# A cross-attention block: the projection's bias put into PSUM by ScalarE, and a new order of the first blocks

## The chip, the core and the metric

The kernel runs on one core of a Trainium2 chip. A core has five engines with a queue each: TensorE (PE; the loading of its stationary operand is shown as PEld), VectorE (DVE), ScalarE (ACT), GpSimd (POOL) and SyncE (SP), which here issues every DMA. Each works through its own instructions in order and waits on semaphores for the others. Matrix products land in PSUM, which has eight banks of 512 float32 per partition; everything else lies in SBUF. The metric is the device time of one launch in microseconds, the median over runs.

## The reference

Two inputs, x (16 batches of 1024 rows, 512 wide) and ctx (16 batches of 64 rows), are normalised and modulated by a conditioning vector, x then attends to ctx with 16 heads of 32, and the result is projected and added to x. All is float32.

```python
def _ada_ln(x, c, W_ss, b_ss):
    mu = mean(x); var = mean((x - mu) ** 2)
    h = (x - mu) / sqrt(var + EPS)
    scale, bias = split(silu(c) @ W_ss + b_ss, 2)
    return (1.0 + scale)[:, None, :] * h + bias[:, None, :]

xq  = _ada_ln(x_q, t_vec, Wss_q, bss_q)
xkv = _ada_ln(x_kv, t_vec, Wss_kv, bss_kv)
q = (xq @ Wq + bq).reshape(B, Lq, nh, dh)
kv = (xkv @ Wkv + bkv).reshape(B, Lkv, 2, nh, dh)
scores = einsum('bqhd,bkhd->bhqk', q, k) / sqrt(dh)
out = einsum('bhqk,bkhd->bqhd', softmax(scores), v)
return x_q + (out @ Wp + bp)
```

## The kernel before

The 16384 rows of x are 32 blocks of 512 rows, two to a batch; NB is 32. A block i goes through these steps, each a function of the kernel:

- `load_x(i)` and `load_residual(i)` bring x twice, into x_i for the normalisation and into r_i for the final sum.
- `q_stats` (DVE), `q_scale` (a square root on ACT, two small POOL operations) and `hidden` (ACT, L277) normalise x_i. `turn` (DVE, L414) transposes it in 32x32 squares into a tile ht, of which there is one, and `move` (16 DMAs, L427) puts the squares where the query product wants them, xt.
- `queries(i, o)` is one of four groups of the query product (PE, L462) into a PSUM bank; `queried` adds the bias on ACT (L479).
- `scores(i, z)` are score products of half of the keys (PE, L490) into two tiles of two banks each, tag "s", of which there are two in all. DVE takes maxima from them (L501), then ACT copies them to SBUF (L508); that frees them.
- `maxima` spreads the maxima over the rows (DVE, L522), `subtract` takes them off (L535, on POOL by default, 128x2048 for each half), `weights` is the exponential (ACT, L541), `sums` adds up (DVE, L546), `inverse` inverts and spreads, `divide` multiplies (POOL, L566).
- `mix` is the product of weights and values (PE, L586), `mixed` or `mixed_halves` its copy to SBUF (ACT, L606 or L654 and L655).
- The projection. Blocks 0 to 2 at first, and the last blocks, use `project` (PE, L613, a bank for each 128 rows) and `projected` (DVE, L626). Blocks 2 to 28 use seven products of halves (`product`, PE, L694) in place of eight, from sums of the rows (`row_sums` on DVE, `last_row_sum` on POOL) and of the weights (`weight_sums`, tile WT); they accumulate in banks 2 and 3 and are added to r in between (`added`, DVE, L708). `residual(i)` has added the projection's bias to r_i before that (POOL, L288, four additions of 128x512).

Four single banks are handed out in turn by `bank`, from the list `ring`; in the loop `ring` has two, and banks 2 and 3 belong to `product`. Two functions for keys and values (`context_features`, `keys`, `value_products`, `value_tiles`) run once for every two batches.

No scheduler moves anything: the order in each queue is the order in which the calls stand in the program. It has three parts: the way in, written out by hand to the products of block 2; a loop over i = 3 to 29, in which parts of blocks i - 2 to i + 3 alternate; and a tail for blocks 30 and 31. In the loop, after `mix(i - 1)` PE has `queries(i + 1, 1)`, then products 1 and 2 of block i - 1; ACT has `mixed_halves(i - 1)` and `hidden(i + 2, (2, 3))`, then the query evacuation.

Of the kernel before, what the change touches and what calls it, by code (L numbers as in the profile page):

```python
# [15 lines left out]
P = 128  # L16
# [4 lines left out]
def cross_attention_block(  # L21
# [319 lines left out]
    def value_products(b):  # L341

        xk = xk_tiles.pop(b)
        pv = bank(f"pv_{b}").rearrange("p (j z f) -> p j z f", j=2, z=2)
        for j in range(2):
            for z in range(2):
                at = j * LKV + z * HK
                for k in range(NC):
                    for c in range(NC):
                        nc.tensor.matmul(  # L350
                            pv[c * 32 : (c + 1) * 32, j, z, :],
                            lhsT=xk[:, k, at : at + HK],
                            rhs=w_kv_sb[:, k, H + c * P : H + (c + 1) * P],
                            start=(k == 0),
                            stop=(k == NC - 1),
                        )
        pv_tiles[b] = pv
# [41 lines left out]
    def query_weights(b):  # L399
        t = qpool.tile([P, NC, H], F32, tag="wq", name=f"wq_{b}")  # L400
        for c in range(NC):
            scale = ss["q"][:, c, b : b + 1]
            if b == 0 and c % 2:
                nc.vector.tensor_scalar_mul(t[:, c, :], w_q_sb[:, c, :], scale)
            else:
                nc.scalar.mul(t[:, c, :], w_q_sb[:, c, :], scale)
        wq_tiles[b] = t
# [119 lines left out]
    def maxima(i):  # L527

        m = small.tile([P, HPC * NJ], F32, tag="m", name=f"m_{i}")
        both(m, m_tiles.pop(i), ALU.max)  # L530
        mb_tiles[i] = spread(i, m, f"mb_{i}", other=i == NB - 1)
# [103 lines left out]
    def half_weights(k, o):  # L635
        return w_p_sb[:, k * HC : (k + 1) * HC, o * HO : (o + 1) * HO]

    def weight_sums():
        t1, t2, t3, t4 = (WT[:, j] for j in range(4))
        nc.vector.tensor_tensor(t1, half_weights(0, 1), half_weights(0, 0), ALU.subtract)  # L640
        nc.vector.tensor_tensor(t2, half_weights(1, 1), t1, ALU.subtract)
        nc.vector.tensor_tensor(t3, half_weights(1, 1), half_weights(0, 1), ALU.subtract)
        nc.vector.tensor_tensor(t4, half_weights(1, 0), t2, ALU.subtract)

    s1_tiles, s2_tiles = {}, {}

# [23 lines left out]
        a12 = half_rows(i, 0, 1)  # L670
        nc.gpsimd.tensor_tensor(a12, a12, s2_tiles[i], ALU.subtract)

    acc = {}

    def product(i, n):

        rows, cols = {
            1: (lambda: half_rows(i, 0, 0), half_weights(0, 0)),
            2: (lambda: half_rows(i, 0, 1), half_weights(1, 0)),
            3: (lambda: half_rows(i, 0, 1), half_weights(1, 1)),  # L680
            4: (lambda: half_rows(i, 1, 1), WT[:, 3]),
            5: (lambda: s1_tiles.pop(i), WT[:, 0]),
            6: (lambda: s2_tiles[i], WT[:, 1]),
            7: (lambda: half_rows(i, 1, 0), WT[:, 2]),
        }[n]
        rows = rows()
        k = 2 if n in (1, 6, 5, 3) else 3
        new = n in (1, 2, 7)
        if new:
            acc[k] = bank(f"pp_{i}_{n}", k)  # L690
        for t in range(2):
            for c in range(HC):

                nc.tensor.matmul(  # L694
                    acc[k][:, t * HO : (t + 1) * HO],
                    lhsT=rows[:, c, t * P : (t + 1) * P],
                    rhs=cols[:, c, :],
                    start=new and t == 0 and c == 0,
                    stop=c == HC - 1,
                    skip_group_check=True,  # L700
                )
# [37 lines left out]
    queries(0, 1)  # L739
    hidden(1, (2, 3))  # L740
    load_x(2)
    for h in range(2):
        scale_shift_rows("kv", h)
    turn(1, range(NT))
    move(1)
    load_x(3)
    load_residual(0)
    load_projection_bias()
    queries(0, 2)
    for h in range(2):  # L750
        scale_shift("kv", 2 * NC, h)
# [6 lines left out]


    scores(0, 0)  # L760
    residual(0)
    value_products(0)
    scores(0, 1)
    turn(2, range(NT))
    move(2)
    load_projection()
    load_context(2)
    load_x(4)
    load_residual(1)
    maxima(0)  # L770
    subtract(0, nc.vector, (0,))
    value_tiles(0)
    subtract(0, nc.vector, (1,))
    queries(1, 0)
    query_weights(1)
    weights(0, 0)
    queries(1, 1)
    weights(0, 1)
    sums(0, 0)
    queries(1, 2)  # L780
    sums(0, 1)
    queries(1, 3)
    inverse(0)
    divide(0)
    scores(1, 0)
    q_stats(3)
    queries(2, 0)
    q_scale(3)
    scores(1, 1)
    maxima(1)  # L790
    queries(2, 1)
    subtract(1)
    queries(2, 2)
    hidden(3, (0, 1))
    mix(0, apart=False)
    mixed(0)
    hidden(3, (2, 3))
    queries(2, 3, spare=True)
    turn(3, (0, 1))
    kv_stats(2)  # L800
    turn(3, (2, 3))
    move(3)
    q_stats(4)
    project(0, 0)
    weights(1, 0)
    sums(1, 0)
    weights(1, 1)
    project(0, 1)
    sums(1, 1)
    q_scale(4)  # L810
    kv_scale(2)
    residual(1)
    project(0, 2, later=True)


    load_x(5)
    scores(2, 0)
    projected(0, 2)
    context_hidden(2)
    inverse(1)  # L820
    divide(1)
    project(0, 3, later=True)
    scores(2, 1)
    projected(0, 3)
    maxima(2)
    queries(3, 0)
    hidden(4, range(NT))
    queries(3, 1)
    queries(3, 2)
    mix(1)  # L830
    mixed(1)
    turn(4, range(NT))
    load_residual(2)
    move(4)
    q_stats(5, (0, 1))
    subtract(2, nc.vector)
    weights(2, 0)
    q_stats(5, (2, 3))
    queries(3, 3)
    weights(2, 1)  # L840
    weight_sums()
    sums(2, 0)
    project(1, 0)
    sums(2, 1)
    inverse(2)
    divide(2)
    q_scale(5)
    residual(2, (0, 1))
    context_features(2)
    project(1, 1)  # L850
    query_weights(2)
    project(1, 2)

# [1 line left out]
    for i in range(3, NB - 2):  # L855
        nxt3 = i + 3 < NB
        kvb = i // 4 * 2 + 2
        kv = i % 4 if kvb < B else None
        if nxt3:
            load_x(i + 3)  # L860
        if kv == 0:
            load_context(kvb)
        if i > 3:
            added(i - 2, 5)
        scores(i, 0)
        if i > 3:
            product(i - 2, 4)
            added(i - 2, 4)
            product(i - 2, 3)
            added(i - 2, 3)  # L870
        else:
            project(i - 2, 3)
            ring[:] = [0, 1]
        scores(i, 1)
        maxima(i)
        subtract(i)
        queries(i + 1, 0)
        load_residual(i)
        hidden(i + 2, (0, 1))
        mix(i - 1)  # L880
        mixed_halves(i - 1)
        hidden(i + 2, (2, 3))
        if kv == 1:
            context_hidden(kvb)
        if nxt3:
            q_stats(i + 3)
        if kv == 0:
            kv_stats(kvb)
        row_sums(i - 1)
        turn(i + 2, range(NT))  # L890
        move(i + 2)
        if not nxt3:
            load_residual(NB - 1)
        queries(i + 1, 1)
        product(i - 1, 1)
        product(i - 1, 2)
        weights(i, 0)
        added(i - 1, 1)
        added(i - 1, 2)
        sums(i, 0)  # L900
        weights(i, 1)
        queries(i + 1, 2)
        last_row_sum(i - 1)
        if i == 3:
            residual(2, (2, 3))
        residual(i)
        product(i - 1, 6)
        product(i - 1, 7)
        sums(i, 1)
        added(i - 1, 6)  # L910
        inverse(i)
        added(i - 1, 7)
        divide(i)
        if nxt3:
            q_scale(i + 3)
        if kv == 0:
            kv_scale(kvb)
        if kv == 2:
            context_features(kvb)
        if kv == 3:  # L920
            keys(kvb)
        queries(i + 1, 3)
        if (i + 2) % BPB == 0 and i + 2 < NB:
            query_weights((i + 2) // BPB)
        if kv == 3:
            value_products(kvb)
            value_tiles(kvb)
        product(i - 1, 5)
# [95 lines left out]
```

## Time and profile before

| what | value |
|---|---|
| median of 3 runs (lowest, highest) | 1095.79 us (1092.36, 1096.22) |
| the profiled execution | 1097.9 us, span of its instructions 1096.1 us |
| mean granted TensorE clock in it | 0.997 |
| busy: PE, DVE, POOL, ACT | 1077.3, 881.9, 746.6, 634.0 us |
| additions of the bias to r, POOL L288 | 128 of 1332 ns, 165.1 us |
| exponential, ACT L541, 128x2048 | 64 of 1915 ns |
| copies of mixed rows, ACT L655, 128x512 | 27 of 596 ns |
| DMA | 145.36 MB, 39.4% of 16 engines' span |

The profile is of one execution. A page gives the busy time of each engine, the chain of work that ended last and the groups of instructions with the mean duration of one. An entry of a timeline has the start and the length in us, engine, line, operation, what it writes and reads, and in brackets the idle time before it and what ended it. Neighbouring instructions of one kind are one entry. An entry of the waits has the waiting engine and line, what it waited for, the sum in us, how often, and the longest. A line of the windows has the stretch, its length, and the busy time of PE, PEld, DVE, ACT and POOL (instructions in brackets), the granted TensorE clock, the share of the DMA engines and GB/s. "Idle" on PE is counted from the modelled end of a product, so a short delay between two products can stand there without a bracket.

### The profile page before, as it was taken

Reading aid. Unit: us, or ns where it says so; the run is one execution under the profiler, and the core shown is the slowest. Engines: PE = TensorE matmul, PEld = TensorE weight load, DVE = VectorE, ACT = ScalarE, POOL = GpSimd, SP = SyncE. Lnnn points to the kernel's source line nnn. Section 1 sums busy time; section 2 is a strip of 40 time slices with the busy share of each in tenths; the row PEclk is TensorE's granted clock in tenths of the full one; section 3 lists DMA queues with packets and bytes.
Section 4 is the critical chain, followed back from the end, with each engine's and each line's share of the span. In section 5 each row is a group of like instructions: output and inputs, shape, how many; then the busy total and the mean of one; then the engine's idle time right before and its main releaser. Section 6 shows DMA issues by size and latency. Waiting matters only on the chain.

```text
span 1096.1 us, 20360 instructions
## 1 busy us (share of the span) xinstructions
PE 1077.3 (98%) x8290; PEld 614.7 (56%) x8290; DVE 881.9 (80%) x1138; ACT 634.0 (58%) x752; POOL 746.6 (68%) x359
## 2 busy tenths in 40 slices
PE   6989999999999999999999999999999999999998
PEld 3533455556655557555566555656656556755533
DVE  4687986888788886898868888688887888697893
ACT  3646754657566573666736677365755657466430
POOL 0065396778857777688758878578875777858830
PEclk9989999999999999999999999999999999999999
DMA  9543333443424442344434434343342443333402
GB/s 354 176 156 107 117 124 126 155 154 116 126 99 145 143 154 88 116 149 141 140 121 138 133 119 140 137 151 119 117 142 105 148 154 131 101 109 102 137 30 87
DMA packets 80525, 145.36 MB, mean 133 GB/s; under 512 B 10504, under 2 KB 10656, under 8 KB 80432
## 3 DMA queue, kind: packets, MB, share of 16 engines
q1 hardware_dynamic: 80432, 144.07, 39.4%
q8 instruction: 65, 1.06, 0.4%
q14 instruction: 28, 0.23, 0.1%
HBM read 77.97 MB, written 33.55 MB: 102 GB/s over the span
## 4 chain that ended last, share of the span: by engine, by line
PE 96%; DVE 2%; DMA 1%; SPq 0%; issue 0%; ACT 0%; DVEq 0%
PE pq L462 40%; PE pp L694 30%; PE po L586 7%; PE ps L490 6%; PE pp L613 6%; PE pv L350 3%; PE pk L322 3%; DMA wss_q<-in_L_xcond_Wss_q_dram 1%; DVE s L535 1%; DVE l L546 0%; PE pss_q L217 0%; PE pkt L302 0%; PE pxt L439 0%; DVE m L501 0%; DVE ht L414 0%; DVE mb L522 0%
## 5 line engine op out<-in xcount | busy, mean ns | idle before, releaser
L462 PE MATMUL pq<-xt,wq 128*128 128x512 f32 x1024 | 468.5, 602 | 1.1 <-DVE vt L363 0.9
L535 POOL TENSOR_TENSOR s<-s,mb 128x2048 f32<-128x2048 f32 x56 | 253.7, 4555 | 154.9 <-DVE mb L522 152.9
L566 POOL TENSOR_TENSOR s<-s,vb 128x2048 f32<-128x2048 f32 x62 | 280.1, 4540 | 84.9 <-DVE vb L522 61.0
L462 PEld LDWEIGHTS pq<-xt,wq 128*128 128x128 f32 x1024 | 189.0, 191 | 246.3 <-issue 241.0
L508 ACT COPY s<-ps 128x1024 f32<-128x1024 f32 x128 | 129.8, 1014 | 195.6 <-DVE m L501 188.3
L479 ACT ACTIVATE qt<-pq,bqs 128x512 f32<-128x512 f32 x128 | 88.0, 689 | 161.7 <-PE pq L462 157.7
L708 DVE TENSOR_TENSOR r<-pp,r 128x512 f32<-128x512 f32 x189 | 126.4, 669 | 68.6 <-PE pp L694 65.9
L288 POOL TENSOR_TENSOR r<-r,b_p_sb 128x512 f32<-128x512 f32 x128 | 165.1, 1332 | 17.8 <-DMA b_p_sb<-in_L_xcond_bp_dram 15.4
L501 DVE TRANSPOSE_TENSOR_REDUCE m<-ps 128x32 f32<-128x1024 f32 x128 | 152.2, 1227 | 27.8 <-PE ps L490 27.8
L546 DVE TRANSPOSE_TENSOR_REDUCE l<-s 128x64 f32<-128x2048 f32 x64 | 146.6, 2300 | 5.5 <-ACT s L541 5.5
L694 PE MATMUL pp<-w_p_sb,ot 128*128 128x256 f32 x648 | 148.7, 379 | 0.0
L541 ACT ACTIVATE s<-s 128x2048 f32<-128x2048 f32 x64 | 122.4, 1915 | 34.2 <-POOL s L535 26.3
L694 PEld LDWEIGHTS pp<-w_p_sb,ot 128*128 128x128 f32 x648 | 123.1, 190 | 28.3 <-issue 6.5
L694 PE MATMUL pp<-WT,ot 128*128 128x256 f32 x432 | 104.9, 386 | 0.0
L694 PE MATMUL pp<-WT,s 128*128 128x256 f32 x432 | 102.8, 381 | 0.0
L694 PEld LDWEIGHTS pp<-WT,s 128*128 128x128 f32 x432 | 81.5, 190 | 32.2 <-issue 20.5
L277 ACT ACTIVATE x<-x,rstdq 128x512 f32<-128x512 f32 x128 | 97.1, 813 | 1.7 <-POOL rstdq L255 1.7
L694 PEld LDWEIGHTS pp<-WT,ot 128*128 128x128 f32 x432 | 79.8, 190 | 32.4 <-DVE r L708 16.8
L246 DVE BATCH_NORM_STATS2 bs<-x 128x6 f32<-128x512 f32 x128 | 84.3, 659 | 2.0 <-DMA x<-in_x_dram 2.0
L414 DVE STREAM_TRANSPOSE ht<-x 128x512 f32<-128x512 f32 x124 | 77.5, 679 | 6.6 <-ACT x L277 6.6
L490 PE MATMUL ps<-qt,kt 32*32 32x512 f32 x2048 | 77.6, 602 | 3.1 <-ACT s L508 2.0
L522 DVE STREAM_TRANSPOSE mb<-m 128x2048 f32<-128x2048 f32 x32 | 74.0, 2311 | 5.0 <-POOL s L566 1.7
(90 smaller groups left out, 887.9 us busy)
## 6 DMA issues: line engine op xcount, KB each, us to landing
x<-in_x_dram SPq DMA_DIRECT2D x32, 1024.0 KB, 5.7
r<-in_x_dram SPq DMA_DIRECT2D x32, 1024.0 KB, 5.4
xt<-ht SPq DMA_DIRECT2D x496, 64.0 KB, 2.0
out_dram<-r SPq DMA_DIRECT2D x54, 512.0 KB, 2.8
out_dram<-r SPq DMA_DIRECT2D x20, 256.0 KB, 2.0
wss_q<-in_L_xcond_Wss_q_dram SPq DMA_DIRECT2D x2, 1024.0 KB, 9.4
ctx<-in_ctx_dram SPq DMA_DIRECT2D x8, 256.0 KB, 5.7
wss_kv<-in_L_xcond_Wss_kv_dram SPq DMA_DIRECT2D x2, 1024.0 KB
```

The lines of the kernel that those rows point to most:

```text
L277: nc.scalar.activation(dst, src, AF.Identity, bias=rstd[:, 1, j : j + 1], scale=rstd[:, 0, j : j + 1])
L288: nc.gpsimd.tensor_add(r_tiles[i][:, t, :], r_tiles[i][:, t, :], b_p_sb)
L462: nc.tensor.matmul(pq.rearrange("p (g n) -> p g n", g=4), lhsT=wq_tiles[b][:, c, o * P : (o + 1) * P], rhs=xt[:, :, c, :], start=(c == 0), ...
L490: nc.tensor.matmul(pss[r // 2][32 * c : 32 * c + 32, r % 2, :], lhsT=kt[rows, c, z * HK : (z + 1) * HK], rhs=qt[rows, c, :], start=True, s ...
L501: nc.vector.tensor_reduce(m_tiles[i][:, z, 2 * e : 2 * e + 2, :], pss[e].rearrange("p r (j a) -> p r j a", a=32), AX.X, ALU.max, apply_tra ...
L508: nc.scalar.copy(s_sb[:, 2 * e : 2 * e + 2, :], pss[e])
L535: eng.tensor_tensor(s_tiles[i, z], s_tiles[i, z], mb_tiles[i], ALU.subtract)
L541: nc.scalar.activation(p, p, AF.Exp, scale=SCALE)
L546: nc.vector.tensor_reduce(l_tiles[i][:, z], s_tiles[i, z].rearrange("p r (j a) -> p r j a", a=32), AX.X, ALU.add, apply_transpose=True,)
L566: eng.tensor_tensor(s_tiles[i, z], s_tiles[i, z], vb, ALU.mult)
L694: nc.tensor.matmul(acc[k][:, t * HO : (t + 1) * HO], lhsT=rows[:, c, t * P : (t + 1) * P], rhs=cols[:, c, :], start=new and t == 0 and c == 0,
L708: nc.vector.tensor_add(r, acc[k].rearrange("p (t h) -> p t h", t=2), r)
```

## The change

In the loop, for i from 4 on, `biased(i - 1)` has ACT copy the bias into banks 2 and 3 before products 1 and 2, which then accumulate on it instead of opening their bank. Bank 2 gets the bias of the second half of the columns, twice side by side, and bank 3 the difference of the two halves, b_diff; what this leaves out is added to a quarter of r by `residual_rest` (POOL), one addition in place of four. Block 2's products, in the round i = 3, still open their banks (`first`), and blocks from 29 on keep `residual`.

The weights' sums and b_diff are computed on POOL, in block 0's scores, instead of on DVE in block 2. On the way in the loads of r_0, the projection's bias and weights are issued earlier, the turning of blocks 2 and 3, sums, projections and the mix of block 1 change places with their neighbours, the subtraction of block 2 goes from DVE to POOL, and the fourth query group of block 2 uses a bank of the ring.

```diff
     def weight_sums():
-        nc.vector.tensor_tensor(t1, half_weights(0, 1), half_weights(0, 0), ALU.subtract)
...
+        nc.gpsimd.tensor_tensor(t1, half_weights(0, 1), half_weights(0, 0), ALU.subtract)
...
+        nc.gpsimd.tensor_tensor(b_diff, b_first, b_second, ALU.subtract)
+    b_first, b_second = b_p_sb[:, :HO], b_p_sb[:, HO:]
+    b_diff = const.tile([P, HO], F32, name="b_diff")
+
+    def twice(b):
+        return b.unsqueeze(1).to_broadcast([P, 2, HO])
+
+    def residual_rest(i):
+        r = r_tiles[i][:, 2:, :HO]
+        nc.gpsimd.tensor_tensor(r, r, twice(b_diff), ALU.add)
+
+    def biased(i):
+        for k, n, b in ((2, 1, b_second), (3, 2, b_diff)):
+            acc[k] = bank(f"pp_{i}_{n}", k)
+            nc.scalar.copy(acc[k].rearrange("p (t h) -> p t h", t=2), twice(b))
...
-    def product(i, n):
+    def product(i, n, first=False):
...
-        new = n in (1, 2, 7)
+        new = n == 7 or first and n < 3
...
     load_x(2)
+    load_residual(0)
+    load_projection_bias()
+    load_projection()
     for h in range(2):
         scale_shift_rows("kv", h)
     turn(1, range(NT))
     move(1)
     load_x(3)
-    load_residual(0)
-    load_projection_bias()
...
     scores(0, 0)
-    residual(0)
-    value_products(0)
-    scores(0, 1)
     turn(2, range(NT))
     move(2)
-    load_projection()
     load_context(2)
     load_x(4)
     load_residual(1)
+    residual(0)
+    weight_sums()
+    value_products(0)
+    scores(0, 1)
     maxima(0)
...
     query_weights(1)
+    queries(1, 1)
     weights(0, 0)
-    queries(1, 1)
+    queries(1, 2)
     weights(0, 1)
     sums(0, 0)
-    queries(1, 2)
+    queries(1, 3)
     sums(0, 1)
-    queries(1, 3)
     inverse(0)
     divide(0)
     scores(1, 0)
+    queries(2, 0)
     q_stats(3)
-    queries(2, 0)
+    queries(2, 1)
     q_scale(3)
     scores(1, 1)
     maxima(1)
-    queries(2, 1)
     subtract(1)
     queries(2, 2)
...
-    queries(2, 3, spare=True)
-    turn(3, (0, 1))
+    queries(2, 3)
+    turn(3, range(NT))
+    move(3)
     kv_stats(2)
-    turn(3, (2, 3))
-    move(3)
     q_stats(4)
     project(0, 0)
     weights(1, 0)
     sums(1, 0)
+    project(0, 1)
     weights(1, 1)
-    project(0, 1)
-    sums(1, 1)
+    residual(1)
+    load_x(5)
     q_scale(4)
     kv_scale(2)
-    residual(1)
-    project(0, 2, later=True)
-    load_x(5)
     scores(2, 0)
-    projected(0, 2)
-    context_hidden(2)
+    sums(1, 1)
     inverse(1)
     divide(1)
-    project(0, 3, later=True)
+    project(0, 2)
+    context_hidden(2)
+    hidden(4, (0, 1))
     scores(2, 1)
-    projected(0, 3)
     maxima(2)
+    subtract(2)
+    hidden(4, (2, 3))
+    project(0, 3)
     queries(3, 0)
-    hidden(4, range(NT))
     queries(3, 1)
     queries(3, 2)
-    mix(1)
-    mixed(1)
     turn(4, range(NT))
     load_residual(2)
     move(4)
-    q_stats(5, (0, 1))
-    subtract(2, nc.vector)
+    mix(1)
+    mixed(1)
+    q_stats(5)
+    queries(3, 3)
     weights(2, 0)
-    q_stats(5, (2, 3))
-    queries(3, 3)
+    project(1, 0)
+    sums(2, 0)
     weights(2, 1)
-    weight_sums()
-    sums(2, 0)
-    project(1, 0)
+    residual(2, (0, 1))
+    project(1, 1)
     sums(2, 1)
     inverse(2)
     divide(2)
     q_scale(5)
-    residual(2, (0, 1))
     context_features(2)
-    project(1, 1)
     query_weights(2)
     project(1, 2)
...
         hidden(i + 2, (2, 3))
+        if i > 3:
+            biased(i - 1)
...
-        product(i - 1, 1)
-        product(i - 1, 2)
+        product(i - 1, 1, first=i == 3)
+        product(i - 1, 2, first=i == 3)
...
-        residual(i)
+        if i < NB - 3:
+            residual_rest(i)
+        else:
+            residual(i)
```

More of the change, by code (lines that the diff above doesn't have):

```diff
@@ L639, in weight_sums @@
         t1, t2, t3, t4 = (WT[:, j] for j in range(4))
-        nc.vector.tensor_tensor(t1, half_weights(0, 1), half_weights(0, 0), ALU.subtract)
-        nc.vector.tensor_tensor(t2, half_weights(1, 1), t1, ALU.subtract)
-        nc.vector.tensor_tensor(t3, half_weights(1, 1), half_weights(0, 1), ALU.subtract)
-        nc.vector.tensor_tensor(t4, half_weights(1, 0), t2, ALU.subtract)
+        nc.gpsimd.tensor_tensor(t1, half_weights(0, 1), half_weights(0, 0), ALU.subtract)
+        nc.gpsimd.tensor_tensor(t2, half_weights(1, 1), t1, ALU.subtract)
+        nc.gpsimd.tensor_tensor(t3, half_weights(1, 1), half_weights(0, 1), ALU.subtract)
+        nc.gpsimd.tensor_tensor(t4, half_weights(1, 0), t2, ALU.subtract)
+        nc.gpsimd.tensor_tensor(b_diff, b_first, b_second, ALU.subtract)
[6 more added lines that the diff above has]
+        nc.gpsimd.tensor_tensor(r, r, twice(b_diff), ALU.add)
+    acc = {}
+    def biased(i):
+        for k, n, b in ((2, 1, b_second), (3, 2, b_diff)):
+            acc[k] = bank(f"pp_{i}_{n}", k)
+            nc.scalar.copy(acc[k].rearrange("p (t h) -> p t h", t=2), twice(b))
     s1_tiles, s2_tiles = {}, {}
@@ L671, in last_row_sum @@
         nc.gpsimd.tensor_tensor(a12, a12, s2_tiles[i], ALU.subtract)
-    acc = {}
-    def product(i, n):
+    def product(i, n, first=False):
         rows, cols = {
```

## The prediction

> **What bounds the kernel now.** I read the page's busy shares first: PE 98%, DVE 80%, POOL 68%, ACT 58%. The chain that ended last agrees: 96% of it is PE. So only what moves PE counts, and the next view is PE's waits.
>
> ```profile
> PE 1077.3 (98%) x8290; PEld 614.7 (56%) x8290; DVE 881.9 (80%) x1138; ACT 634.0 (58%) x752; POOL 746.6 (68%) x359
> ```
>
> ```profile
> PE ps L490 <- ACT s L508: 2.0, 1, 2.0
> PE pq L462 <- DVE vt L363: 0.9, 1, 0.9
> PE ps L490 <- DVE kt L330: 0.8, 1, 0.8
> PE ps L490 <- ACT qt L479: 0.3, 1, 0.3
> ```
>
> The reader should see that four waits after the first loads make 4.0 us, each occurring once; the 27 rounds of the loop show none. Then I took the timeline of PE and the windows of 2 us (span, then busy time of PE, PEld, DVE, ACT, POOL, then the granted clock).
>
> ```profile
> 70.91 2.95 PE L490 MATMUL ps<-qt,kt 32*32 32x512 f32 x32 [1.98 <-ACT s L508]
> 73.79 9.75 PE L462 MATMUL pq<-xt,wq 128*128 128x512 f32 x16
> 83.48 3.00 PE L586 MATMUL po<-s,vt 32*32 32x512 f32 x64
> 86.40 3.70 PE L462 MATMUL pq<-xt,wq 128*128 128x512 f32 x8
> ...
> 74.00:76.00 2.00, 2.00 (x3) 0.97 (x4) 1.56 (x4) 0.34 (x2) 2.00 (x1) 0.50 0.19 72
> 76.00:78.00 2.00, 2.00 (x3) 0.67 (x2) 1.41 (x3) 1.88 (x2) 2.00 (x2) 0.50 0.00 0
> ```
>
> "Busy" hides loss here: behind the 1.98 us wait the clock is half from 72 to 79 us, and two query groups take 9.7 us instead of 7.1. Counting work at full pace (queries 3.44 us a group in a row, 3.63 behind a small-tile group; a block of scores 1.07; mix 2.28), 40.5 to 86.4 us holds some 35 us of work, so about 11 us are lost, and 0.4 more at 138 us. That is all the way in can give.
>
> Last, a round of the loop, PE and then ACT:
>
> ```profile
> 183.57 3.70 PE L462 MATMUL pq<-xt,wq 128*128 128x512 f32 x8
> 187.10 3.62 PE L694 MATMUL pp<-w_p_sb,ot 128*128 128x256 f32 x16
> ...
> 183.75 1.01 ACT L654 COPY ot<-po 128x1024 f32<-128x1024 f32 x1 [0.26 <-PE po L586]
> 184.66 0.60 ACT L655 COPY ot<-po 128x512 f32<-128x512 f32 x1
> 185.14 1.53 ACT L277 ACTIVATE x<-x,rstdq 128x512 f32<-128x512 f32 x2
> 187.31 0.69 ACT L479 ACTIVATE qt<-pq,bqs 128x512 f32<-128x512 f32 x1 [0.63 <-PE pq L462]
> ...
> 217.40 0.81 ACT L277 ACTIVATE hk<-ctx,rstdk 128x512 f32<-128x512 f32 x1
> ...
> 58.50 0.39 PEld L462 LDWEIGHTS pq<-xt,wq 128*128 128x128 f32 x2 [1.53 <-PE pq L462]
> ...
> 58.71 3.59 PE L462 MATMUL pq<-xt,wq 128*128 128x512 f32 x8 [0.90 <-DVE vt L363]
> ```
>
> Mix ends at 183.64 here. PE then has one query group, 183.57 to 187.10, before products 1 and 2. ACT meanwhile drains the mixed rows and normalises two tiles, ending at 186.67. Product 1 follows with no gap, and that is where the change puts its copies.
>
> **What the Trainium skill says.** "ScalarE: Activation LUTs", section "What ACT_TABLE_LOAD costs", gives an instruction with immediate operands 186 ns + 0.833 ns per element, 612 ns for 512, and an overlap of 93 ns between neighbours; the trace has 596 ns for L655 (out of PSUM), about 105 ns of overlap, and 1283 ns for a table load as the page says. The same page's "Step-by-step" says that writing PSUM is quicker than writing SBUF; nothing in this trace writes PSUM from ACT. "TensorE: Matmul & The Clock Gate", Part 1, has the clock fall to half after an idle window of about 3.4 us; here a window with 1.98 us idle did, for 7 us. "SBUF — State Buffer", section "Who interferes with whom", says a VectorE operation with two SBUF inputs and a GpSimd one that reads SBUF exclude each other: agreed, the DVE subtractions of block 0 take 3.14 and 2.70 us beside POOL's additions, 2.23 (4.46 for two) without, and the four additions 9.08 us instead of 4.96.
>
> **The change, part by part.**
>
> *Loads.* r_0, the projection's bias and weights go on SP's queue before move(1). They add 2.36 MB behind a queue that is full until 30 us; at the 400 GB/s of that stretch they are in by 36 to 37 us. The 16 pieces of move(1) are bound by SP's issue (32.5 to 43.9 us) and needed at 47.3, so I cost it nothing; the cover is about 1.5 us.
>
> *Block 0's additions and the weights' sums on POOL.* POOL is idle from 37.7 to 53.1 us. Four additions at 1.24 us, four sums of the same 512 elements at 1.24 to 1.29, and b_diff, about 0.7: 10.7 us, done at 48.5. Block 0's DVE subtractions come after that and shrink from 5.84 to 4.46 us. DVE loses four sums, 2.7 us, at 123 us, and the two subtractions of block 2 (4.5 us), which go to POOL.
>
> *Turn(2) ahead of block 0's second maxima.* It needs move(1)'s buffer free (45.9 us), so it runs 45.9 to 48.4; the maxima follow to 50.75, the spread maximum to 53.3 (54.5 before), subtractions to 58.5 (61.0), with the value tiles at 56.25 between, in time for PE's query group at 57.8: the 0.9 us wait goes. ACT's second exponential ends at 61.3, the last query evacuation at 62.1, so scores(1,0) wait about 0.9 and end at 63.2 (65.2 before). Two query groups now cover the maxima of block 1: slots free at 69.1 and 70.2, PE needs them at 70.3 and 70.8. The 1.98 us wait goes, barely.
>
> *What is late next.* PE gets to mix(0) at 75.0 instead of 83.5, but ACT only evacuates query group (2,2) at 77.2, behind the copies of block 1's scores: 1.6 us waiting. Query group (2,3), no longer in a spare bank, waits for the first mixed copy: it starts at 79.35 instead of 86.40. Projections and scores of block 2 then run without a wait (score slots free at 93.4 and 94.55, needed at 94.6), mix(1) at 109.6 finds its divide done at 108.0, and scores(3,1) wait 1.25 for DVE, which frees slots at 131.6 and 132.8. Mix(2) ends at 139.2 instead of 145.33: **-6.1 us**. I accept 2.5 to 8.5.
>
> *Bias copies.* In 26 rounds (i = 4 to 29) ACT writes two banks of 512 elements after the second normalisation, and product 1 no longer opens its bank but waits for the first copy. Start: an ACT instruction put there already starts 2.93 us after mix ends (217.40 against 214.47). Duration, not in the trace: from 0.42, the bare element rate (what 512 elements more cost from L655 to L654), to 0.71, the one-pointer L406; I take 0.60. It ends 3.53 after mix. PE holds the weight load too while it waits: at 58.39 the value tiles were done, the load began at 58.50, the product at 58.71; elsewhere a wait ends 0.05 us after its cause. So product 1 starts 0.05 + 0.205 us after the copy, at 3.79, against 3.47 now: 0.32 us (0.14 to 0.43), with neither end below nothing. PE has no slack behind it: 26 x 0.32 = **+8.3 us** (3.6 to 11.2). The second copy ends 4.03 after mix, and product 2 is due at 5.5. Behind it on ACT the next evacuation slips 0.3 us (about 1 with context work), but the second exponential waits for POOL at 8.5 after mix anyway and the divide has 2.4 us to spare (209.7 against 212.1): nothing.
>
> *POOL in the loop.* residual() shrinks from 4.96 to about 1.3 us for 26 blocks; divide waits for DVE's vb there: nothing. The tail keeps its order: nothing.
>
> Sum: -6.1 + 8.3 = +2.2 us on the profiled execution, 1096.1 us of span within 1097.9. That execution lies 2.1 above the median of 1095.79; I apply the difference to the median: **1098 us**.
>
> **The rivals.**
> A, the copies are hidden: ScalarE's write to PSUM is so quick, or the weight load so little held, that product 1 starts on time. For it, the page's sentence; against, even at 0.42 us the wait comes out 0.14. Only the way in counts: 1095.8 - 6.1 = 1089.7, faster.
> B, slower: the copy is long. At L277's 0.81 us it ends 3.74 after mix, the wait is 0.53, 26 of them 13.8: 1103.5. It decides from (6.1 + 5.5) / 26 = 0.45 us a round, thus a copy of 0.73. Against it, copies without a pointer take 0.60.
> C, the way in gives little: the 1.6 us wait at mix(0) is near the 1.98 that halved the clock before. Another 7 us at half clock cost 3.4: 1095.8 - 2.7 + 8.3 = 1101.4. Waits of 0.8 and 0.9 did not trigger it.
>
> **How the numbers follow.** My forecast 0.48, A 0.27, B 0.11, C 0.14. Half a per cent, 5.5 us, is about what a measurement of this kernel can tell from no change: faster is below 1090.3, slower above 1101.3. Faster takes 0.7 of A and 0.05 from the forecast where the way in gives 8 and copies cost little: 0.24. Slower takes most of B, half of C and a sliver of the forecast: 0.18. The forecast's own range is 1094 to 1102; to leave out no more than two in ten I go from 1088, most of A, to 1103, C and the near half of B.
>
> **What would show it.** Right: mix(2) ends near 139 us; the round of 30.83 us becomes 31.15; between the query group and product 1 PE shows a start 0.3 us late, put down to the bias copy on ACT, with a copy near 0.6 us; waits near 75 us for ACT and no half clock. Wrong if rounds keep 30.83 us (A), if they exceed 31.28 (B), or if the clock row shows 0.50 near 77 us (C). A transfer of move(1) or r_0 late, or a wait at a place where I have under 0.5 us of cover (70.3, 94.6 us), would move the way in by 1 to 2 us.

## The result, and the profile after

The changed kernel takes 1100.33 us (median of 6 runs, 1099.69 to 1101.45), the kernel before in the same comparison 1096.23 (6 runs, 1092.36 to 1097.20): a ratio of 1.0043, 95% interval 1.0028 to 1.0058. That is 4.1 us longer. The loss is clear of noise, but the median lies inside the half per cent that the prediction called no measurable change (the interval reaches a little beyond it), and inside its range; 1098 was forecast. The profiled execution took 1099.69 us, with a span of 1097.9 us.

The page's first part, for the kernel after (busy time of each engine, share of the span, instructions), and the chain that ended last, by line:

```profile
PE 1079.0 (98%) x8290; PEld 612.1 (56%) x8290; DVE 874.1 (80%) x1132; ACT 656.7 (60%) x804; POOL 661.0 (60%) x288
...
PE 92%; DMA 3%; DVE 2%; ACT 1%; SPq 1%; issue 0%; DVEq 0%
PE pq L462 38%; PE pp L715 31%; PE po L586 7%; PE ps L490 6%; PE pp L613 6%; PE pv L350 2%; PE pk L322 2%; DMA w_kv_sb<-in_L_xcond_Wkv_dram 1%; DMA w_p_sb<-in_L_xcond_Wp_dram 1%; DVE m L501 1%; SPq L144 1%; DMA x<-in_x_dram 1%; SPq L427 1%; DVE vb L522 0%; DVE l L546 0%; ACT s L541 0%
```

POOL lost 85.6 us of work and DVE 7.8, ACT gained 22.7, and none of it is the bound: the time went up. The new name to see is the load of w_p, which the change issued earlier: it is now in the chain, ahead of L427, the pieces of move.

PE's waits after the first loads, in the kernel after (sum in us, how often, the longest):

```profile
PE pq L462 <- DMA xt<-ht: 1.7, 1, 1.7
PE po L586 <- ACT qt L479: 1.2, 1, 1.2
PE ps L490 <- DVE kt L330: 0.8, 1, 0.8
PE ps L490 <- ACT s L508: 0.7, 1, 0.7
PE ps L490 <- ACT qt L479: 0.3, 1, 0.3
```

The 1.98 us for score slots and the 0.9 us for the value tiles are gone, as the prediction has it. A wait of 1.65 us for block 1's transposed input is new, and so is the predicted one at mix(0), 1.19 us where 1.6 was said. The waits sum to 4.7 us, against 4.0 before. Where they lie is in the timeline of PE:

```profile
48.10 14.18 PE L462 MATMUL pq<-xt,wq 128*128 128x512 f32 x32 [1.65 <-DMA xt<-ht]
...
71.73 1.30 PE L490 MATMUL ps<-qt,kt 32*32 32x512 f32 x32
72.96 3.70 PE L462 MATMUL pq<-xt,wq 128*128 128x512 f32 x8
76.59 1.11 PE L586 MATMUL po<-s,vt 32*32 32x512 f32 x24
78.90 2.15 PE L586 MATMUL po<-s,vt 32*32 32x512 f32 x40 [1.19 <-ACT qt L479]
...
139.50 2.35 PE L586 MATMUL po<-s,vt 32*32 32x512 f32 x64
```

The last entry is mix(2); it ends at 141.85 us, where the kernel before had 145.41 in its profiled execution:

```profile
143.06 2.35 PE L586 MATMUL po<-s,vt 32*32 32x512 f32 x64
```

The way in is thus 3.6 us shorter between these two executions. The clock stayed full on the whole of it, behind the wait at mix(0) too:

```profile
76.00:78.00 2.00, 1.71 (x26) 0.20 (x24) 1.62 (x4) 1.77 (x2) 2.00 (x2) 1.00 0.04 8
78.00:80.00 2.00, 1.10 (x35) 0.48 (x37) 2.00 (x1) 2.00 (x4) 0.22 (x2) 1.00 0.00 0
```

(Columns of the windows as in the prediction; the 1.00 is the granted clock.) The round that the prediction showed, now with PE, the weight loads and ACT; mix ends at 180.08:

```profile
180.01 3.70 PE L462 MATMUL pq<-xt,wq 128*128 128x512 f32 x8
183.65 3.72 PE L715 MATMUL pp<-w_p_sb,ot 128*128 128x256 f32 x16
...
183.65 3.32 PEld L715 LDWEIGHTS pp<-w_p_sb,ot 128*128 128x128 f32 x16 [0.77 <-ACT pp L665]
...
181.58 1.52 ACT L277 ACTIVATE x<-x,rstdq 128x512 f32<-128x512 f32 x2
183.00 0.59 ACT L665 COPY pp<-b_p_sb 128x512 f32<-128x512 f32 x1
183.52 0.59 ACT L665 COPY pp<-b_diff 128x512 f32<-128x512 f32 x1
184.03 0.69 ACT L479 ACTIVATE qt<-pq,bqs 128x512 f32<-128x512 f32 x1
```

PE's entry has no bracket, because the end of the query group is modelled. The wait shows on PEld: the first weight load begins at 183.65, 0.05 us after the first copy ends (3.515 us after mix). Product 1 begins 3.57 us after mix instead of 3.47, its first step lasts 0.10 us longer than usual, and everything behind it is 0.205 us late. So a round of 31.04 us follows, where it was 30.83. Both other kinds of round, 31.27 and 38.23 us before, lengthen by the same. From the end of mix(2) to the end of the span it is 1097.9 - 141.85 = 956.05 us, against 1096.1 - 145.41 = 950.69 before: 5.36 us, which is 26 times 0.206. Nothing is left over for the tail.

Loop +5.4 and way in -3.6 make +1.8 between the two profiled executions, as their spans have it. The medians differ by 4.1. That gap, and what in the change makes each term, is what the experiments are about.

### The profile page after: what moved, and what is told of

The parts are those of the page before. It is cut to its first block, busy times and chain, and to the rows that moved or that the text cites. A ratio compares the mean times of both kernels' runs of the same rounds, so it can differ in the third digit from the quotient of the medians.

```text
span 1097.9 us, 20355 instructions
## 1 busy us (share of the span) xinstructions
PE 1079.0 (98%) x8290; PEld 612.1 (56%) x8290; DVE 874.1 (80%) x1132; ACT 656.7 (60%) x804; POOL 661.0 (60%) x288
## 4 chain that ended last, share of the span: by engine, by line
PE 92%; DMA 3%; DVE 2%; ACT 1%; SPq 1%; issue 0%; DVEq 0%
PE pq L462 38%; PE pp L715 31%; PE po L586 7%; PE ps L490 6%; PE pp L613 6%; PE pv L350 2%; PE pk L322 2%; DMA w_kv_sb<-in_L_xcond_Wkv_dram 1%; DMA w_p_sb<-in_L_xcond_Wp_dram 1%; DVE m L501 1%; SPq L144 1%; DMA x<-in_x_dram 1%; SPq L427 1%; DVE vb L522 0%; DVE l L546 0%; ACT s L541 0%
## 5 line engine op out<-in xcount | busy, mean ns | idle before, releaser
L535 POOL TENSOR_TENSOR s<-s,mb 128x2048 f32<-128x2048 f32 x58 | 262.6, 4553 | 160.9 <-DVE mb L522 158.8
L715 PE MATMUL pp<-w_p_sb,ot 128*128 128x256 f32 x648 | 151.4, 384 | 0.0
L541 ACT ACTIVATE s<-s 128x2048 f32<-128x2048 f32 x64 | 121.9, 1910 | 21.0 <-POOL s L535 16.3
L490 PE MATMUL ps<-qt,kt 32*32 32x512 f32 x2048 | 76.6, 600 | 1.8 <-DVE kt L330 0.8
L586 PE MATMUL po<-s,vt 32*32 32x512 f32 x2048 | 76.1, 599 | 1.2 <-ACT qt L479 1.2
```

The lines of the kernel that those rows point to most:

```text
L490: nc.tensor.matmul(pss[r // 2][32 * c : 32 * c + 32, r % 2, :], lhsT=kt[rows, c, z * HK : (z + 1) * HK], rhs=qt[rows, c, :], start=True, s ...
L535: eng.tensor_tensor(s_tiles[i, z], s_tiles[i, z], mb_tiles[i], ALU.subtract)
L541: nc.scalar.activation(p, p, AF.Exp, scale=SCALE)
L586: nc.tensor.matmul(po[c][32 * r : 32 * r + 32, :], lhsT=vt[rows, z, 32 * r : 32 * r + 32], rhs=p[rows, r, :], start=(z == 0), stop=(z == 1),)
L715: nc.tensor.matmul(acc[k][:, t * HO : (t + 1) * HO], lhsT=rows[:, c, t * P : (t + 1) * P], rhs=cols[:, c, :], start=new and t == 0 and c == 0,
```

## The experiments

All ratios below are to the kernel before, run on the same chip in the same comparison (1094.72 to 1094.94 us there, 34 to 75 runs each).

**One part of the change at a time.** The changed kernel with the loop of the kernel before, so the new way in alone:

```diff
-        if i > 3:
-            biased(i - 1)
...
-        product(i - 1, 1, first=i == 3)
-        product(i - 1, 2, first=i == 3)
+        product(i - 1, 1, first=True)
+        product(i - 1, 2, first=True)
...
-        if i < NB - 3:
-            residual_rest(i)
-        else:
-            residual(i)
+        residual(i)
```

> The changed way in with the loop of before: no bias copies, products 1 and 2 open their banks, residual() in full. If the two parts add up (my theory): a round back at 30.83 us, product 1 at 3.47 us after mix, 26 x 0.205 = 5.3 us below the changed kernel, about 1095 us, a ratio to before of 0.997; mix(2) still ends near 142 us. If the loss sits in the new way in (rival: what it triggers costs the loop), a round stays above 30.9 us or the time stays near 1100 us.

Measured: 1095.41 us (21 runs), ratio 1.0007 (1.0000 to 1.0014). Rounds are 30.83 us again and product 1 begins at 3.47. Mix(2) ends at 141.71, as in the changed kernel. The 3.6 us by which this beats the profiled execution of the kernel before would be a ratio of 0.9967; in the medians the new way in is worth nothing.

The other half, the new loop behind the old way in (the kernel before with `biased`, `residual_rest` and b_diff on DVE, placed in the loop as in the change):

```diff
+        nc.vector.tensor_tensor(b_diff, b_first, b_second, ALU.subtract)
...
+        if i > 3:
+            biased(i - 1)
...
-        residual(i)
+        if i < NB - 3:
+            residual_rest(i)
+        else:
+            residual(i)
```

> The way in of before (one more VectorE subtraction, b_diff, of 256 columns) with the new loop: bias copies and residual_rest. My theory: a round of 31.04 us and before + 5.3 us, about 1101.5 us, a ratio of 1.005. Rival, that the new order of the way in is what loses: a ratio of 1.000 within 0.002.

Measured: 1099.61 us (5 runs), ratio 1.0042 (1.0026 to 1.0058), the whole loss of the change. Its rounds lasted 31.04 us. In its profiled execution the old way in ran at full clock, and mix(2) ended at 138.63 us. That is 6.8 us earlier than in the profiled execution of the kernel before, with the same way in. Not all of it is the clock: the first query group of block 0, which comes behind the first loads, started 3.0 us earlier too. Here it is in this kernel, with mix(2), and then in the kernel before:

```profile
16.72 3.70 PE L462 MATMUL pq<-xt,wq 128*128 128x512 f32 x8
...
136.28 2.35 PE L586 MATMUL po<-s,vt 32*32 32x512 f32 x64
```

```profile
19.71 3.70 PE L462 MATMUL pq<-xt,wq 128*128 128x512 f32 x8
```

None of the edits touches what comes before this entry, yet in the thirteen profiled executions it starts anywhere from 16.60 to 19.71 us, and latest in the kernel before. So the yardstick was off by two things: late first loads and the half clock.

**Is it the place of the copies?** The changed kernel with the copies moved ahead of the first half of the normalisation, and so ahead of the mix:

```diff
         load_residual(i)
+        if i > 3:
+            biased(i - 1)
         hidden(i + 2, (0, 1))
         mix(i - 1)
         mixed_halves(i - 1)
         hidden(i + 2, (2, 3))
-        if i > 3:
-            biased(i - 1)
```

> The changed kernel with the two bias copies put on ACT ahead of the first pair of normalisations, so before mix and not after it. If the place of the copies is what costs (my theory): product 1 back at 3.47 us after mix, a round of 30.83 us, about 1095 us, though ACT works as long as before. If the loss is the additional work on ACT or the accumulation onto a written bank: a round stays at 31.04 us, about 1100 us. Copies of mixed rows start some 0.7 us later; the rows' sums on DVE have more than that to spare.

Measured: 1095.18 us (13 runs), ratio 1.0003 (0.9994 to 1.0011), rounds of 30.83 us, product 1 at 3.47. The same copies cost nothing where ACT has time before mix ends.

**Which of the two copies?** The changed kernel without the first copy of each round; the bias of one bank is left out of the sums:

```diff
-        for k, n, b in ((2, 1, b_second), (3, 2, b_diff)):
+        for k, n, b in ((3, 2, b_diff),):
...
-        new = n == 7 or first and n < 3
+        new = n in (1, 7) or first and n < 3
```

> The changed kernel without the first of the two bias copies of a round: product 1 opens its bank itself, the second copy (the one of b_diff) stays where it is. The bias of one bank is left out of the sums. Theory (only the copy ahead of product 1 is waited for, the second lies behind product 1 and the query product): rounds of 30.83 us, product 1 at 3.47 us after the mix, ratio to the kernel before about 1.000, as with the way in alone. Rival (ScalarE's queue as a whole is what is late: the second copy delays the query's bias and the exponentials, and these reach TensorE): rounds of 30.95 to 31.04 us and a ratio of 1.002 or more.

Measured: rounds of 30.83 us, product 1 at 3.47 after mix, with the second copy in place (starting 2.92 after mix). The second copy costs nothing. The ratio is 1.0014 (1.0004 to 1.0023), a little above the expected 1.000; its way in is that of the changed kernel, whose interval with the old loop reaches 1.0014.

**How does the hold grow?** The first copy made twice into the same bank:

```diff
             nc.scalar.copy(acc[k].rearrange("p (t h) -> p t h", t=2), twice(b))
+            if k == 2:
+                nc.scalar.copy(acc[k].rearrange("p (t h) -> p t h", t=2), twice(b))
```

> The changed kernel as it is, with the first bias copy of each round made twice into the same bank. Theory (product 1's weight load is held to the end of the copies into its bank, and everything behind it on TensorE follows): the copy itself lasts 0.59 us and the next one begins 0.515 us after it, so product 1 begins near 4.08 instead of 3.57 us after the mix, rounds last 31.04 + 0.515 = 31.56 us, 26 rounds add 13.4 us, ratio to the kernel before 1.0165. Rival (part of the hold is absorbed behind it by the waits of the round): rounds of 31.1 to 31.4 us, ratio 1.006 to 1.012.

Measured: 1115.3 us (4 runs), ratio 1.0199 (1.0179 to 1.0219); rounds of 31.61 us. PE's waits in this kernel, and its timeline at one round, mix ending at 179.77:

```profile
PE pp L717 <- ACT pp L667: 13.2, 26, 0.6
```

```profile
179.70 3.70 PE L462 MATMUL pq<-xt,wq 128*128 128x512 f32 x8
183.96 3.72 PE L717 MATMUL pp<-w_p_sb,ot 128*128 128x256 f32 x16 [0.56 <-ACT pp L667]
...
182.70 0.59 ACT L665 COPY pp<-b_p_sb 128x512 f32<-128x512 f32 x1
183.32 0.59 ACT L667 COPY pp<-b_p_sb 128x512 f32<-128x512 f32 x1
183.84 0.58 ACT L665 COPY pp<-b_diff 128x512 f32<-128x512 f32 x1
```

A longer hold now has a bracket of its own, once in each of the 26 rounds. The second copy into the bank starts 0.62 us after the first instead of 0.52, perhaps because both write the same bank; that is why the rounds are 31.61 and not the 31.56 expected. In most rounds product 1 begins 4.14 us after mix, 0.67 late, and what follows is 0.77 late. The difference is 0.10 us, the same as with one copy. So the law of the hold has two terms: the end of the copy plus 0.05 us against the 3.47 us at which product 1 would begin anyway, and 0.10 us once for the weight load that could not run ahead. With no first copy it is 30.83, with one 31.04, with two 31.61.

**The loads on the way in.** The changed kernel with the load of w_p put back behind move(2), and the weights' sums behind the residual of block 2, since they need it:

```diff
     load_projection_bias()
-    load_projection()
...
     move(2)
+    load_projection()
...
-    weight_sums()
...
     residual(2, (0, 1))
+    weight_sums()
```

> The changed kernel with the projection's weights loaded where they were before (behind move(2)) and the weights' sums on POOL behind the first half of block 2's residual. If the eighth piece of move(1), queued behind that load, is what delays the way in (my theory): that piece goes out near 36 us instead of 39.7, the 1.65 us wait of the query product near 46 us falls below 0.3, mix(2) ends near 139.8 instead of 141.8 us, and the time is 2 us lower, about 1098.3 us. Rival, that the residual's load or the turn of block 2 delays it: the wait stays above 1 us. The loop keeps 31.04 us a round either way.

Measured: 1097.3 us (6 runs), ratio 1.0030 (1.0019 to 1.0042), with rounds of 31.04. SP's waits in the changed kernel show what this removes:

```profile
SPq L427 <- DMA w_p_sb<-in_L_xcond_Wp_dram: 3.5, 1, 3.5
```

The eighth of move(1)'s 16 pieces waited on SP until the megabyte of w_p had landed, at 39.7 us: SP's DMAs use eight semaphores in turn here, and an issue waits for the eighth DMA before it. The last piece was issued by 46.25 us (43.88 before) and turn(2), which needs the same buffer, began at 47.98. With w_p late, turn(2) begins at 44.96 and the query product waits 0.76 us instead of 1.65. How much the load costs depends on how early the execution is otherwise (starts of PE's first query group and of block 1's query groups, and the end of mix(2), in us):

| profiled execution | first group | block 1's groups | mix(2) ends |
|---|---|---|---|
| w_p early: the changed kernel | 18.98 | 48.10 | 141.85 |
| w_p early: new way in, old loop | 16.92 | 47.73 | 141.71, half clock for 3 us |
| w_p late | 16.78 | 45.00 | 140.07, half clock for 4 us |
| w_p late, early copies (below) | 17.14 | 44.67 | 138.49 |
| the kernel before | 19.71 | 47.27 | 145.41, half clock for 7 us |
| old way in, new loop | 16.72 | 44.12 | 138.63 |

With w_p early, block 1's query groups start at 47.6 to 48.1 us in all five such executions without filling, though PE's first group varies from 16.6 to 19.0: the landing of w_p sets them. In the other rows, and in the filled kernel before (further down), they follow the first group by 27.4 to 28.2 us. So an execution whose first loads come early loses its lead to w_p. Mix(2) ends at 140.07 with w_p late, though this execution met something else, in the windows of PE (stretch, its length, PE's busy time, granted clock, DMA share, GB/s):

```profile
76.00:78.00 2.00, 2.00 (x41) 1.00 0.00 0
78.00:80.00 2.00, 2.00 (x5) 0.54 0.00 0
80.00:82.00 2.00, 2.00 (x4) 0.60 0.00 0
```

Behind the wait of 1.19 us at mix(0) the clock fell to half for nearly 4 us. It is what the prediction's rival C described, at its place, in an execution of a neighbouring kernel.

**Both repairs.** Early copies and late w_p together:

> The changed kernel with both repairs: the bias copies ahead of hidden(i+2, (0, 1)) and so ahead of the mix, and the load of w_p back behind move(2), the weights' sums behind residual(2, (0, 1)). Theory (the loop's hold of 0.205 us a round and the place of the w_p load are the two losses, and they add): rounds of 30.83 us, mix(2) ends near 140, so a span near 140.1 + 950.7 = 1090.8 us, a ratio to the kernel before of 0.997 to 0.998. Rival (what the way in gains is taken back by a spell of half clock somewhere in it, whatever the order of loads): mix(2) ends at 142 or later and the ratio is 0.999 to 1.001.

Measured: 1092.17 us (22 runs, 1090.11 to 1094.30), ratio 0.9982 (0.9974 to 0.9991). Rounds of 30.83, mix(2) at 138.49, no stretch under full clock on the way in. Faster than the kernel before and, by 0.6%, than the changed one. The difference of the ratios to early copies alone, 0.0021, is 2.3 us for the place of one load and of the sums that need it; the two ratios come from two comparisons, and their intervals do not overlap. With the copies in their late place the same move gave 1.0030 instead of 1.0043, 1.4 us, with intervals that do overlap. PE's timeline where the changed kernel waited 1.65 us:

```profile
44.67 10.54 PE L462 MATMUL pq<-xt,wq 128*128 128x512 f32 x24
55.43 3.59 PE L462 MATMUL pq<-xt,wq 128*128 128x512 f32 x8 [0.22 <-PE pq L462]
```

**What is the half clock worth in the kernel before?** In the three comparisons of these experiments the kernel before ran 144 times. Its mean clock was 0.997 in 92 runs, which averaged 1095.3 us, and 1.000 in 12, which averaged 1091.4: 4 us apart with not an instruction changed, though early first loads may be part of that. In the profiled execution the half clock followed the idle 1.98 us before scores(1,1). To see whether that idle time brings it, I left everything else as it was and filled it with two products of 128x512, whose results the query group that owns the bank overwrites:

```diff
+    filled = bank("pq_2_1")
+    for _ in range(2):
+        nc.tensor.matmul(filled, lhsT=wq_tiles[0][:, 0, :P], rhs=wq_tiles[0][:, 0, :],
+                         start=True, stop=True)
     scores(1, 1)
     maxima(1)
-    queries(2, 1)
+    queries(2, 1, pq=filled)
```

> The kernel before, with two products of 128x512 (0.89 us each) ahead of scores(1, 1), where TensorE waited 1.98 us in the profiled execution; their results are overwritten by the query product that owns the bank. Theory (this idle stretch brings the half clock behind it, which costs 3 to 4 us in about two executions of three): clocks of 0.999 and 1.000 instead of 0.997, median 2 to 3.5 us below that of the kernel before, ratio 0.997 to 0.998. Rival (the half clock comes with something else): clocks of 0.997 in two executions of three, ratio 0.9995 to 1.0005.

Measured: 1092.12 us (22 runs), ratio 0.9981 (0.9972 to 0.9989). Its clock was 0.999 or 1.000 in all 22 runs, which still spread over 2.9 us. PE's timeline, with the filling as L793:

```profile
66.82 1.88 PE L793 MATMUL pq<-wq 128*128 128x512 f32 x4
68.82 2.22 PE L492 MATMUL ps<-qt,kt 32*32 32x512 f32 x32
70.97 7.13 PE L464 MATMUL pq<-xt,wq 128*128 128x512 f32 x16
```

Work that is thrown away makes the kernel faster: the two query groups behind it take 7.13 us, where they took 9.75, and mix(2) ends at 139.96. It settles the yardstick. At full clock the old way in ends near 138.6 to 140.0 (two executions), and the new one at 141.85. Counted from the start of the first query group, to leave the first loads out, mix(2) ends 121.9 and 121.6 us later in these two (125.7 in the profiled execution of the kernel before), 122.9 in the changed kernel and 121.4 with both repairs. So at full clock the new order with w_p late gains 0.2 to 0.6 us on the old, by single executions, and the filled kernel before (0.9981) is as fast as the one with both repairs (0.9982). What the single moves of the new order give was not taken apart.

**The same filling in the new way in.** Here the gaps are the wait for the transposed input and mix(0). On the changed kernel with early copies, whose profiled execution waited 4.0 us for the transposed input (`fill=n` puts n products of 128x512 ahead):

```diff
-    queries(1, 0)
+    queries(1, 0, fill=7)
...
-    mix(0, apart=False)
+    mix(0, apart=False, fill=2)
```

> The changed kernel with early bias copies (way in unchanged), and idle stretches of TensorE in the way in filled with products whose results are overwritten: seven of 128x512 ahead of the first query product of block 1 (it waited 4.0 us for its transposed input in the earlier run) and two ahead of mix(0) (1.2 us). Theory (an idle stretch of some us brings the half clock that most executions show behind it): mean clock 1.000 in nearly all runs, no stretch under full clock before 100 us, median 1.5 to 3 us below that of the kernel with early copies alone, ratio 0.997 to 0.999. Rival (the half clock comes with the rise in load, or at random, and not with the idle time): clocks of 0.997 and 0.998 as before, or the fillers themselves run at half clock, ratio 1.000 to 1.002.

Measured: 1096.28 us (22 runs), ratio 1.0020 (1.0010 to 1.0029). The filling was mis-sized: a product of this type is two records in the trace, 0.89 us together, so seven took 6.28 us and not the 3.1 meant, and made PE late themselves. The clocks were 0.998 in 3 runs and 0.999 or 1.000 in 19, where the kernel without filling had 0.997 or 0.998 in 11 of 13. With three and one instead of seven and two:

> The changed kernel with early bias copies and shorter fillers than before: three products of 128x512 (0.89 us each, since a product of this type takes two passes of 0.44) ahead of the first query product of block 1 and one ahead of mix(0), less than the waits there. Theory (idle time brings the half clock): clock of 0.999 and 1.000 in most executions, median 1 to 2.5 us below the kernel with early copies alone, ratio 0.998 to 0.9995. Rival: clocks of 0.997 and 0.998, ratio 1.000 to 1.001.

Measured: 1094.59 us (14 runs), ratio 1.0006 (0.9996 to 1.0016); clock 0.999 or 1.000 in 13 of 14. The half clock went, the gain expected from that did not come. The profiled execution of the new way in with the old loop suggests why. There PE waited 3.34 us, the clock was half from 48 to 51 us, and the first query groups lost 1.5 us:

```profile
47.73 15.67 PE L462 MATMUL pq<-xt,wq 128*128 128x512 f32 x32 [3.34 <-DMA xt<-ht]
63.32 1.98 PE L490 MATMUL ps<-qt,kt 32*32 32x512 f32 x32
65.23 7.13 PE L462 MATMUL pq<-xt,wq 128*128 128x512 f32 x16
...
78.94 1.47 PE L586 MATMUL po<-s,vt 32*32 32x512 f32 x33 [0.82 <-ACT qt L479]
```

Against the kernel after (48.10, 62.21, 64.67, 78.90 for the same entries) it is 0.4 us ahead at the start, 1.1 behind at the scores, 0.6 behind at the next queries and level at mix(0): the wait of 0.34 us at the scores is gone and that at mix(0) is 0.82 instead of 1.19. The loss lies in waits for ACT that stood there anyway. In this stretch of the new way in that half clock was covered; behind the old one's 1.98 us it was not. A longer one is covered in part only: with early copies and no filling the wait was 3.96 us, the clock half for 6 us, and mix(2) ended at 143.16, against 141.70 with this shorter filling.

Last, fillings in the kernel with both repairs, one product ahead of the first query group and two ahead of mix(0):

> The kernel with both repairs and fillers: one product of 128x512 ahead of the first query product of block 1 and two ahead of mix(0), their results overwritten. Theory (idle time brings the half clock): clock 1.000 in nearly all runs, ratio below that of the kernel with both repairs by 0.001 to 0.003, at 0.995 to 0.997. Rival (the idle time is not what brings it): same ratio as without fillers within 0.001, and clocks as there.

Measured: 1092.06 us (22 runs), ratio 0.9978 (0.9970 to 0.9985), not told apart from 0.9982 without them. The expected 0.995 to 0.997 did not come: without filling this kernel already ran at 0.999 or 1.000 in 17 of 22 runs.

## Why the prediction was right, and where it was not

The total was right to 0.2%, and its two terms were both too large, in opposite directions. That their errors cancelled is luck: the loop cost 3.0 us less than said, and the way in gained 4.9 us less or more.

**Bias copies, +8.3 us: mechanism right, size off.** The copy starts 2.93 us after mix, as read from the trace of before, lasts 0.59 us (0.60 taken) and ends at 3.515 (3.53). PE follows it after 0.05 us. The mis-sized term is the held weight load: 0.205 us were added, 0.104 it costs. So 0.205 us a round in place of 0.32, and 26 of them are 5.3 us. The prediction had read 0.21 us between the start of the load and the start of the product behind the value tiles. That it did not take off what a load and a product overlap anyway is the likely reason, not tested. "ScalarE: Activation LUTs", section "Step-by-step", with its quicker writes to PSUM, does not show: 0.587 to 0.590 us into PSUM against 0.593 for L678, which writes SBUF; but L678 reads PSUM and these copies read SBUF, so the two differ in more than where they write.

**Second copy, POOL and tail, nothing: right.** Without the first copy the second one costs nothing, and the span behind mix(2) grows by 26 holds and no more.

**Way in, -6.1 us: failed, in two steps.** The first is the part on the loads: "so I cost it nothing; the cover is about 1.5 us". The working looked at bandwidth, and at SP's issue of move(1), but not at what an issue waits for. The queue did move some 400 GB/s until 36 us, as reckoned, yet w_p counted as landed only at 39.7, not by 36 to 37; why its last part took so long is open. It held one piece for 3.5 us, and turn(2) began 2.1 us later than the predicted 45.9. Block 0's chain kept that delay: mix(0) was reached at 76.6 and not 75.0, query group (2,3) at 80.97 and not 79.35, mix(1) at 111.6 and not 109.6. Mix(2) ended at 141.85 and not 139.2; the 0.6 us more that came behind mix(1) is not explained. Putting the load back gives 2.3 us, as the runs with early copies show. The rest of that chain was read well: POOL's additions and sums ended at 47.7 (48.5 said), the additions alone took the 4.96 us said, the two subtractions of block 0 2.29 and 2.28 us (4.46 said for both), and both named waits went.

The second is "I apply the difference to the median". The profiled execution lay 2.1 us above the median, and that had been written down; what was not seen is why. Its first query group was the latest of all thirteen profiles, a delay that the changed kernel, whose block 1 starts with the landing of w_p, hides in part; and it had 3.4 us of half clock, which belongs to many runs of the kernel before and not to all. A difference to such an execution is no difference to the median. The 3.6 us between the two profiled executions came out as 1.2 in the comparison of medians (4.1 less the loop's 5.3), and as none in the run of the way in alone.

**The rivals.** A (hidden copies) and B (a long copy) fell: rounds of 31.04 us lie between 30.83 and 31.28. C named something that does happen, but it is not what took the gain of the way in. The changed kernel's two runs at a clock of 1.000 took 1099.69 and 1100.21 us, its four at 0.998 from 1100.10 to 1101.45. The half clock did not come at mix(0) in the profiled execution of the changed kernel, it came there in that of the kernel with late w_p, and behind the wait for the transposed input in two others. "TensorE: Matmul & The Clock Gate", section "HAM oscillation — how this bites in real kernels", puts it down to idle gaps of more than about 3.4 us. The runs agree that idle time brings it, since filling took it away, and not on the length: 1.98 and 1.19 us, each in one execution and next to products on 32x32 tiles, were followed by it.

What stays open: which gaps trigger it. At the wait for the transposed input 1.65, 2.35 and 2.67 us brought no half clock in the profiled executions, 3.34 brought half for 3 us and 3.96 for 6 us; ahead of mix(0) 1.2 us brought it in one execution and not in four others; ahead of scores(1,1) 1.98 us brought it, and 1.70 us, in the old way in with the new loop, did not. One profile of each kernel cannot settle that.

## What to carry to other kernels

Before a few microseconds of a way in are priced from one profile, look at the clock row and at the clocks of all runs: where the kernel's own executions differ by a half-clock stretch, count the predicted gain from the full-clock path and price the stretch apart. Compare executions from the first product on, since the first loads alone moved them by up to 3 us here. A copy that opens an accumulation costs its end against the product's own start, plus the weight load that can no longer run ahead, in every round; put where its engine had time before the mix, it was free here. When a load is moved up a queue, ask which later issues wait for it to land, and not only for the bandwidth.

## What the runs showed of the hardware

- A weight load held by its product's wait for another engine cost 0.10 us beyond the wait and the 0.05 us to wake: the same with holds of 0.10 us (the changed kernel) and 0.67 us (the first copy made twice) at product 1.
- Two neighbouring ScalarE copies of 128x512 overlap by 0.07 us when they write different banks (starts 0.52 us apart) and not when they write the same one (0.62 us apart, 0.59 us each); whether the bank or the program's own order does it is open.
- Discarded TensorE work of 1.9 us in an idle stretch of 1.98 us made the kernel before 2.8 us faster, with 0.999 or 1.000 as the clock of all 22 runs, where 92 of 144 without it had 0.997.
- On SP's queue of this program an issue waits for the landing of the eighth DMA before it; a 1 MB load held a 64 KB piece for 3.5 us. The eight semaphores are the program's, so this need not be the chip's rule.
- The same first loads let TensorE's first query group start anywhere from 16.60 to 19.71 us in thirteen executions, though nothing ahead of it differed.
